# Paged attention on one Trainium2 core: opening with register-addressed copies of the conditions' weights, mixed input transposed by VectorE, last projection in two halves

## The chip, the cores and the metric

The kernel runs on one core of one Trainium2 chip. The metric is the device time of an execution in microseconds (us), lower is better. A core has five engines that run side by side and wait for each other through semaphores: TensorE (PE, with its weight loads PEld), VectorE (DVE), ScalarE (ACT), GpSimd (POOL) and SyncE (SP). SP, ACT and POOL also issue DMA copies, each in its own queue.

## What is computed

Two layers with residuals, on 64 sequences of 32 tokens and 512 channels, all in 32-bit floats. The first mixes the 32 tokens of a sequence with one of 16 weight tables of 32x32, chosen by the sequence's condition. The second is attention with 32 query heads and 8 key/value heads of 128 over a paged cache of 512 keys, of which the first `cache_seqlens` are valid, plus the 32 new tokens.

```python
x = x + einsum('bct,bcd->bdt', x, weights[condition])
q, k, v = x @ Wq.T, x @ Wk.T, x @ Wv.T          # q: 32 heads, k and v: 8
q, k = rope(rmsnorm(q)), rope(rmsnorm(k))
k_all = concat(k_cache[block_table], k); v_all = concat(v_cache[block_table], v)
probs = softmax(where(valid, q @ k_all * scale, -1e30))
x = x + (probs @ v_all) @ Wo.T
```

## The kernel before

The work is cut into 32 steps. A step is four sequences (128 token rows, BT = 4) with one half of the heads: steps 0 to 15 are all rows with heads 0 to 15 (`st.hh` = 0), steps 16 to 31 the same rows with the other heads. A step has four batches (its sequences), a batch four slots (its key/value heads), so a step has slots 0 to 15. In each slot PE makes the scores of one head group (`scores`, L570), ACT their exponential, and PE the product with the values of the slot before (`values`, L626). Between these lie, slot by slot, pieces of the next step: its key projection in slot 3 and query projections in 4 to 7, its v projection in 13 (`pieces`, L866), and the output projection of the step before in 8 and 9 (`out_proj`, L513). Two steps ahead, in slots 14 and 15, the rows are mixed and turned:

- `x1_c` (L359): PE multiplies the rows with `bd`, which holds the four sequences' weight tables on its diagonal (`pmix`), and DVE adds the product to the rows (`acc`).
- `x1_b` (L366): PE transposes the mixed rows in four blocks of 128x128 into PSUM (`px1t`), ACT copies them to `x1t`, the operand of the projections, and stores `x1t` in DRAM (`x1t_d`), from where the second half of the steps loads it (`x1_t`, L353).

The order of SP's queue and of PE's work is written by hand: they take what they have to do in the order of the program, over the whole kernel. In the opening (L766 to L864) that holds for all engines. SP issues the cached keys page by page (64 KB each, 16 a batch, two batches ahead, L294), the spreading of the turned queries (`spread`, L466), the loads and stores of the rows, and the weights; each batch's page numbers are first loaded into registers (L286). POOL gathers the cached values (`fetch`, L314, 256 KB each), which ACT masks (L334). The rotation of queries and keys (`norm_rope`, L412) runs on ACT, DVE and POOL; its products use the work buffer with tag `w1`, of which there is one.

The opening loads the condition of each row, from which DVE computes a row index, and POOL gathers the first step's weight tables with it (`w_sel`, L772). The index rows of the value gathers (`cached_rows`, L160) need `pages_at` and `lens_at`, which POOL loads after three weight loads. The first angles (`angles`, L133) are computed before the first mix, the second ones after `cached_rows`. `keep_warm` (L788) keeps PE busy with products of an identity. At the end, `in_range` (L1013) counts the usable denominators within the last output projection, and a branch runs an exact version if any is out of range.

## Time and profile before

| what | us |
|---|---|
| median of 3 runs | 2170.74 (2169.95 to 2174.28) |
| the profiled execution | 2166.54 |
| its span, first to last instruction | 2164.8 |
| PE busy | 2145.4 (99% of the span) |
| DVE / ACT / POOL busy | 1196.6 / 863.0 / 805.5 |

The profile is of one execution. Times in its views are counted from the first instruction. L12 is line 12 of the kernel. The chain of waits follows the work that ended last back to what released it. A matmul of 128x512 in 32-bit floats stands in it as two records of 0.43 us; a transpose of 128x128 as one of 0.11.

### The profile page before, as it was taken

To read this page: it belongs to the slowest core of one execution; us is meant where nothing else is said; L and a number is where in the kernel's file an instruction comes from. 1 tells how busy PE (TensorE), PEld (TensorE's weight loads), DVE (VectorE), ACT (ScalarE), POOL (GpSimd) and SP (SyncE) were. 2 spreads that over 40 slices of the span, in tenths; PEclk is the share of its full clock that TensorE was granted. 3 is DMA by queue.
4 is the path that set the end of the run, shared out by engine and by line. 5 is a ranking of instruction groups with operands and counts; after the bars stand their busy time and mean duration, and the time that the engine had idled before them with its cause. 6 is when DMAs were issued, how large, how long until landed. Compare 5 with 4: busy or idle time off the path is not lost.

```text
span 2164.8 us, 41582 instructions
## 1 busy us (share of the span) xinstructions
PE 2145.4 (99%) x12990; PEld 1497.4 (69%) x12990; DVE 1196.6 (55%) x2884; ACT 863.0 (40%) x1576; POOL 805.5 (37%) x1009
## 2 busy tenths in 40 slices
PE   8999999999999999999999999999999999999998
PEld 5766777667776677766777766777667777667775
DVE  5666555665455564555654565644655545556442
ACT  3444444444433343333443333433334433334441
POOL 4433333433333343333433334333334333334330
PEclk9999999999999999999999999999999999999999
DMA  8665565555655556556766855565555555555651
GB/s 250 188 165 160 157 169 160 143 159 158 173 153 153 154 156 173 156 151 190 229 181 178 207 161 162 164 177 156 155 144 168 165 167 165 147 159 162 172 158 59
DMA packets 386839, 357.47 MB, mean 165 GB/s; under 512 B 54480, under 2 KB 316640, under 8 KB 386608
## 3 DMA queue, kind: packets, MB, share of 16 engines
q1 hardware_dynamic: 341616, 212.74, 35.1%
q0 software_dynamic: 41984, 137.71, 22.3%
q10 hardware_dynamic: 3008, 4.25, 0.5%
q8 instruction: 106, 1.74, 0.3%
q14 instruction: 125, 1.02, 0.2%
HBM read 302.59 MB, written 12.58 MB: 146 GB/s over the span
## 4 chain that ended last, share of the span: by engine, by line
PE 97%; DVE 1%; DMA 1%; ACT 0%; issue 0%; POOL 0%; DVEq 0%; ACTq 0%
PE po_x L632 22%; PE ps_x L574 21%; PE pout_x L520 20%; PE pp_q_x L407 20%; PE pp_v_x L407 5%; PE pp_k_x L407 5%; PE pnv_x L616 2%; PE psn_x L592 1%; PE pmix_x L363 1%; DMA pages_at<-in_pages_v_dram 1%; PE px1t_x L371 0%; DMA cond<-in_cond_dram 0%; PE pt_x L451 0%; ACT sq_q_x L417 0%; ACT q_cols_x L491 0%
## 5 line engine op out<-in xcount | busy, mean ns | idle before, releaser
L321 POOL DMA_INDIRECT raw_x<-in_vc_dram,v_row x512 | 539.6, 1054 | 821.5 <-ACT v_x L334 757.0
L582 ACT ACTIVATE pr_x<-ps_x 128x512 f32<-128x512 f32 x512 | 305.7, 597 | 822.7 <-PE ps_x L574 819.3
L632 PEld LDWEIGHTS po_x<-v_x,pr_x 128*128 128x128 f32 x4096 | 515.7, 192 | 123.9 <-issue 112.5
L632 PE MATMUL po_x<-v_x,pr_x 128*128 128x129 f32 x4096 | 550.6, 278 | 0.0
L407 PE MATMUL pp_q_x<-wq_x,x1t_x 128*128 128x512 f32 x1024 | 462.2, 594 | 0.0
L520 PE MATMUL pout_x<-wo_x,ot_x 128*128 128x512 f32 x1024 | 450.2, 593 | 0.0
L574 PE MATMUL ps_x<-q_cols_x,kh_x 128*128 128x128 f32 x3072 | 406.0, 275 | 1.6 <-ACT q_cols_x L491 1.6
L574 PEld LDWEIGHTS ps_x<-q_cols_x,kh_x 128*128 128x128 f32 x3072 | 376.3, 192 | 18.0 <-issue 14.5
L334 ACT ACTIVATE v_x<-raw_x,valid 128x512 f32<-128x512 f32 x512 | 363.2, 716 | 13.4 <-DMA raw_x<-in_vc_dram,v_row 13.2
L520 PEld LDWEIGHTS pout_x<-wo_x,ot_x 128*128 128x128 f32 x1024 | 190.0, 191 | 214.0 <-issue 213.8
L567 DVE COPY kh_x<-k_t_x 128x512 f32<-128x512 f32 x506 | 206.8, 418 | 194.6 <-PE ps_x L574 153.5
L407 PEld LDWEIGHTS pp_q_x<-wq_x,x1t_x 128*128 128x128 f32 x1024 | 185.8, 191 | 184.8 <-issue 184.8
L650 DVE TENSOR_TENSOR nv_x<-po_x,nv_x 128x258 f32<-128x258 f32 x256 | 108.6, 424 | 309.4 <-PE po_x L632 294.0
L424 POOL TENSOR_TENSOR rs_q_x<-ms_q_x,minus_half 128x4 f32<-128x4 f32 x128 | 140.0, 1094 | 168.9 <-DVE ms_q_x L422 168.9
L417 ACT ACTIVATE sq_q_x<-pp_q_x 128x512 f32<-128x512 f32 x128 | 76.4, 597 | 266.2 <-PE pp_q_x L407 179.3
L574 PE MATMUL ps_x<-q_last_x,kh_x 128*128 128x128 f32 x1024 | 135.3, 275 | 0.0
L528 DVE TENSOR_TENSOR acc_x<-pout_x,acc_x 128x512 f32<-128x512 f32 x32 | 22.2, 692 | 199.3 <-PE pout_x L520 199.3
L574 PEld LDWEIGHTS ps_x<-q_last_x,kh_x 128*128 128x128 f32 x1024 | 124.6, 192 | 0.0
L407 PE MATMUL pp_v_x<-wv_x,x1t_x 128*128 128x512 f32 x256 | 115.2, 593 | 0.0
L407 PE MATMUL pp_k_x<-wk_x,x1t_x 128*128 128x512 f32 x256 | 115.1, 593 | 0.0
L653 DVE TENSOR_TENSOR o_x<-nv_x,rden 128x256 f32<-128x256 f32 x256 | 108.8, 425 | 6.2
L421 DVE TENSOR_REDUCE ms_q_x<-sq_q_x 128x4 f32<-128x512 f32 x128 | 86.3, 674 | 45.4 <-ACT sq_q_x L417 44.8
(107 smaller groups left out, 1464.8 us busy)
## 6 DMA issues: line engine op xcount, KB each, us to landing
k_t_x<-in_kt_dram SPq DMA_DIRECT2D x2048, 64.0 KB
q_cols_x<-rows_x SPq DMA_DIRECT2D x360, 80.0 KB
q_last_x<-rows_x SPq DMA_DIRECT2D x120, 80.0 KB
raw_x<-in_vc_dram,v_row POOLq DMA_INDIRECT x512, 4.2
wo_x<-in_wo_dram SPq DMA_DIRECT2D x32, 256.0 KB
acc_x<-in_x_dram SPq DMA_DIRECT2D x16, 256.0 KB
x1t_d<-x1t_x ACTq DMA_DIRECT2D x16, 256.0 KB
acc_d<-acc_x SPq DMA_DIRECT2D x16, 256.0 KB
```

What stands on the lines that cost most here:

```text
L321: nc.gpsimd.indirect_dma_start(out=raw.rearrange("p g d -> p (g d)"), out_offset=None, in_=vc, in_offset=bass.IndirectOffsetOnAxis(ap=v_ro ...
L334: nc.scalar.activation(v_bufs[b % 2][:, c, :, 0:D], raw, AF.Copy, scale=ok)
L407: nc.tensor.matmul(pp, st.x1t[:, c, :], w[:, c, :], start=(c == 0), stop=(c == KC - 1))
L421: nc.vector.tensor_reduce(ms, sq, AX.X, ALU.add)
L424: nc.gpsimd.tensor_tensor(rs, ms, minus_half, ALU.pow)
L520: nc.tensor.matmul(st.po, st.ot[:, i, :], wt["o", st.hh, i // 4][:, i % 4, :], start=(i == 0), stop=(i == QH - 1),)
L567: last["dve"] = nc.vector.tensor_copy(k, ba.k_raw[:, :, g, :]).ins
L574: nc.tensor.matmul(ps[:, c, :], ba.k[g][:, c * P : (c + 1) * P], queries(ba, g), start=True, stop=True,)
L582: last["act"] = nc.scalar.activation(pr, ps, AF.Exp, scale=SCALE).ins
L632: nc.tensor.matmul(ba.po[:, g % 2, :], ba.pr[g][:, c, :], ba.v_t[:, c, g, :], start=(c == 0), stop=(c == VC - 1),)
L650: nc.vector.tensor_tensor(t, ba.po, t, ALU.add)
L653: nc.vector.tensor_tensor(ba.o[:, both, :], t[:, :, 0:D], rd.unsqueeze(2).to_broadcast([P, 2, D]), ALU.mult,)
```

## The change

- **Opening, conditions.** `cond_0`, its index and the gather of `w_sel` go. ACT's first copy is now the condition row, its second the page numbers. SP loads all 16 weight tables (`w_all`, 64 KB) after the first rows. DVE loads the first step's four conditions into registers and copies four 32x32 blocks addressed by them. The tables of step 1 are loaded by SP instead of ACT.
- **Opening, order of loads.** The second quarter of wq goes from POOL to SP. `pages_at` and `lens_at` go from POOL to ACT. The fourth quarter of wq and the second batch of keys come after step 1's tables.
- **Opening, order of work.** The first mix comes before the angles. The second angles are split: DVE's part (`reduced`) before the first query projection, ACT's part (`sines`) after it, followed by an exponential of one column. Some projections, gathers, copies, scores and values change places. The first `x1t` is stored by POOL, later. There are fewer warming products (10, 4 and 3 instead of 16, 6 and 4).
- **Steps 2 to 15.** The mixed rows are no longer transposed by PE. DVE turns their 32x32 blocks (`x1_turn`), SP writes them to `x1t_d` with four DMAs, which put the blocks in place in pieces of 32 floats, and at the start of the next step SP loads `x1t` back, after the first four key pages of a batch and before the other twelve.
- **End.** The last output projection is made in two halves of 256 columns, each with its own addition and store; `in_range` is called within the first.

```diff
@@ steps_of: x1 @@
         def x1_b(st):
             if st.hh:
                 return
+            if not by_tensor(st):
+                return x1_turn(st)
...
             nc.scalar.copy(st.x1t, pm)
-            nc.scalar.dma_start(x1t_d[st.t], st.x1t.rearrange("p c q -> p (c q)"))
+            if st.n or exact:
+                keep_x1t(st, nc.scalar)
...
+        def x1_turn(st):
+            turned = work.tile([P, KC * BT, S], F32, tag="w1", name=f"x1w_{st.name}", bufs=1)
+            nc.vector.transpose(turned, st.acc.rearrange("p (j d) -> p j d", d=S))
+            kept = x1t_d[st.t].rearrange("(j d) (c b x) -> b d c j x", d=S, b=BT, x=S)
+            for b in range(BT):
+                nc.sync.dma_start(
+                    kept[b],
+                    turned[b * S : (b + 1) * S, :, :].rearrange("p (c j) x -> p c j x", c=KC),
+                )
@@ out_proj @@
-                nc.vector.tensor_tensor(st.acc, st.po, st.acc, ALU.add)
+                nc.vector.tensor_tensor(st.acc[:, cols], st.po[:, cols], st.acc[:, cols], ALU.add)
                 if exact or st is steps[-1]:
-                    store(st)
+                    store(st, cols)
@@ opening: loads @@
-            nc.scalar.dma_start(cond_0, cond[:, 0:1])
-            nc.vector.tensor_scalar(cond_0, cond_0, float(S), row, ALU.mult, ALU.add)
-            nc.gpsimd.dma_start(pages_sb, pages)
+            nc.scalar.dma_start(cond_row, cond.rearrange("(i s) t -> s t i", s=S)[0:1])
+            nc.scalar.dma_start(pages_sb, pages)
...
         x1_a(first)
+        w_all = work.tile([S, NCOND, S], F32, tag="pr", name="w_all", bufs=3)
+        nc.sync.dma_start(w_all, w_cond.rearrange("(n s) e -> s n e", s=S))
         load_w("q", 0, 0)
+        load_w("q", 0, 1)
         nc.scalar.dma_start(lens_sb, lens)
         nc.scalar.dma_start(freq, inv_freq.partition_broadcast(P))
...
         load_w("k", 0, eng=nc.gpsimd)
-        load_w("q", 0, 1, eng=nc.gpsimd)
+        nc.scalar.dma_start(pages_at, pages_v)
+        nc.scalar.dma_start(lens_at, lens_row.partition_broadcast(P))
         load_w("q", 0, 2, eng=nc.gpsimd)
         batch = Batch(first, 0)
         load_w("v", 0)
         x1_a(second)
-        load_w("q", 0, 3)
-        later = Batch(first, 1)
...
         keep_warm(WARM)
+        number = conditions(0, mybir.EngineType.DVE)
+        for i in range(BT):
+            blk = slice(i * S, (i + 1) * S)
+            nc.vector.tensor_copy(
+                bd[blk, blk], w_all[:, bass.ds(number[i], 1), :].rearrange("p o e -> p (o e)")
+            )
+        x1_c(first)
+        load_cond_weights(1)
+        load_w("q", 0, 3)
+        later = Batch(first, 1)
         positions()
         angles(0, trig)
-        for i in range(BT):
-            nc.vector.tensor_copy(bd[blk, blk], w_sel[blk, :])
-        x1_c(first)
-        keep_warm(6)
+        keep_warm(4)
         x1_b(first)
-        load_cond_weights(1, nc.scalar, mybir.EngineType.Activation)
-        keep_warm(4)
+        keep_warm(3)
         rot_tables(first)
...
         cached_rows(pages_at, lens_at)
-        angles(TRIG, trig)
-        for c in range(RAW):
-            fetch(0, c)
-        fetch(0, RAW, tag="pn", bufs=1)
+        reduced(TRIG, trig)
         q_a(first, 0)
+        sines(TRIG, trig)
+        nc.scalar.activation(early, half_pi, AF.Exp)
+        fetch(0, 0)
+        fetch(0, 1)
         k_a(first)
+        fetch(0, 2)
+        keep_x1t(first, nc.gpsimd)
         q_a(first, 1)
+        fetch(0, RAW, tag="pn", bufs=1)
@@ opening: further on @@
-        k_b(first)
+        new = v_product(first)
+        q_b(first, 1)
         for c in (0, 1):
             batch.fill(c)
             fetch(1, c)
-        v_a(first)
-        q_b(first, 1)
+        v_copy(first, new)
...
         x1_b(second)
-        scores(batch, 2)
...
         q_b(first, 3)
+        scores(batch, 2)
         scores(batch, 3)
...
         values(batch, 1)
+        values(batch, 2)
         new_values(first, 2)
@@ loop over the steps @@
+                back = bt == 0 and ahead and not ahead.hh
...
+                        NPP // 4 if back else NPP // 2 if bt == BT - 1 else NPP,
+                    if back:
+                        x1_t(ahead)
+                        for load in after.pages_left:
+                            load()
...
-                        if beyond:
+                        if beyond and beyond.hh:
                             x1_t(beyond)
@@ end @@
-        out_proj(steps[-1], slice(0, QH), in_range)
+        out_proj(steps[-1], slice(0, QH), slice(0, HID // 2), in_range)
+        out_proj(steps[-1], slice(0, QH), slice(HID // 2, HID))
```

## The prediction

> **What bounds the kernel now.** I read the page's busy shares first (PE 99%), then the windows by stage, since an average over the run hides the two ends.

> ```profile
> 0.00:62.00 62.00, 52.14 (x269) 34.34 (x270) 32.87 (x94) 23.71 (x52) 26.11 (x46) 0.94 0.80 232
> 62.00:2100.00 2038.00, 2038.00 (x12406) 1424.07 (x12405) 1146.19 (x2742) 821.73 (x1494) 770.03 (x952) 1.00 0.59 166
> ```

> The columns are the stretch in us, its length, busy time of PE, weight loads, DVE, ACT and POOL, the granted clock, the DMA engines' share and GB/s. From 62 us on TensorE has no idle time at all and full clock; DVE is at 56%, ACT 40%. So in that stretch only PE work that goes away, or a new PE stall, changes the time. What is idle on PE lies in the first 62 us, where the DMA engines are at 0.80, and in the last 10. The chain of waits tells why the opening idles:

> ```profile
> 7.71 11.25 DMA pages_at<-in_pages_v_dram
> ...
> 19.06 0.35 DVE v_row L164
> ...
> 23.06 0.31 ACT sin L150
> ...
> 24.00 0.49 ACT sq_q_x L417
> ...
> 42.77 3.73 issue
> ...
> 59.13 1.54 PE pnv_x L616 x16
> ```

> The copy of pages_at stands behind 3 MB of weights in POOL's queue, lands at 18.96, and holds DVE (index rows, then the second pair of angles), which holds the sines on ACT, which hold the first square, although its projection was over at 18.9. From there DVE's norm-and-rotate chain (3.65 us for each of q0, k, q1, q2) and ACT set the pace. The step's own part, in the same view around a step boundary, and the SP queue beside it in the timeline:

> ```profile
> 233.33 0.86 PE pmix_x L363 x2
> ...
> 235.97 0.44 PE px1t_x L371 x4
> ...
> 247.37 3.44 PE pp_k_x L407 x8
> ```
> ```profile
> 227.09 0.53 SPq L351 DMA_DIRECT2D acc_x<-in_x_dram  x1
> 229.05 8.44 SPq L294 DMA_DIRECT2D k_t_x<-in_kt_dram  x16
> ```
> ```profile
> 241.77 5.93 SPq L294 DMA_DIRECT2D k_t_x<-in_kt_dram  x11
> ```

> The four transposes of the mixed input cost PE 0.44 us a step, and 11.4 us later the key projection needs the result. SP is late at this point: it issues the 16 key pages of slots 12 and 13 one every 0.54 us until 237.5, past the end of slot 15. The end:

> ```profile
> 2151.61 3.65 PE pout_x L520 x8
> ...
> 2155.27 0.69 DVE acc_x L528
> ```

> [...] The new stores write 128 B pieces. The trace before has no such write; its 128 B reads (bd) took 12 ns a packet in the trace's packet records, the 512 B key pages 27, the 2 KB stores of x1t_d 87. [...] beside the 1 MB of wq, three small copies issued by ACT within 0.9 us landed at 3.82 (cond), 5.27 (lens) and 7.02 (freq)[...]. [...] STREAM_TRANSPOSE of 128x512 takes 0.70 us here. [...] 0.66 in the window 10 to 15 us, after PE's 3.2 us of idling before pmix.

> **Steps 2 to 15: the transposes.** 14 steps lose four PE transposes: 14 x 0.44 = **-6.2 us**, all on the path, since PE is never idle there. A cross-check: a first-half step takes 67.13 us (projection of the output at 205.44, next at 272.57), a second-half step 65.83 (1405.96 to 1471.79); the difference of 1.30 is pmix 0.86 plus 0.44. ACT loses its copy (0.58) and one store. DVE gains 0.70 us a step; it was idle from 236.5 to 240.3, which hides it. The tile shares tag w1 with the rotation's; the next user is the key's rotation at 252, long after the stores have read it. The x1t buffer that the load fills was last read by v's projection, over by 231.6.

> What is added on SP: four stores (64 KB in 512 pieces each), and in the next step the load, which waits for all four; behind it on SP wait 12 key pages. Those have room: SP's queue sat idle on its buffers from 262.5 to 269.7 in this step, and the keys are needed a batch later. The load itself has not. From 237.5: stores at 0.6 each (the spread copies of L471, 80 KB each, come every 0.62; bounds 0.35, as the old store, and 0.9) 2.4; the page-number load 1.1; four pages 2.1, which makes 243.1. The stores have landed by then if they take under 3.8 us after the last issue at 239.3 (the old store was issued at 237.18 and SP, which waited for it, went on at 241.77: at most 4.6). The load of 256 KB: a gather of the same size lands in a median 4.1 us in this stretch, of which 1.0 is its own issue; 3.1, bounds 2.4 and 4.1. So x1t is there at 246.2, and k's projection wants it at 247.37 - 0.44 = 246.9. Bounds: 2.4 us early (0.35, 2.4), 2.0 late (0.9, so a last issue at 240.2, a store of 4.6, 4.1). I take it as in time in most steps and late in some, 0.3 us on the mean: 14 x 0.3 = **+4.2 us**.

> **The opening.** The condition row is now ACT's first copy, so it lands like cond did, at 3.9. DVE's register load isn't in the trace: SP's of the same row takes 0.30, ACT's 0.51; I take 0.5, with all of DVE queued behind it and pmix waiting. Four 32x32 copies of 0.17 with their register moves, 1.0. The weight table itself (64 KB, second on SP) should land with the condition row. So pmix starts at 5.9 instead of 10.07. Then freq binds: fourth on ACT's queue, beside SP's two 1 MB loads and POOL's, at 9.5 (bounds 7.0, as now, and 11). Angles 2.3 on DVE, sines 0.9 and the x1t copy 0.6 on ACT: first projection at 13.5 instead of 15.34. It may run at half clock for a time, +1. pages_at and lens_at leave POOL's queue for the fifth and sixth place on ACT's, 16 (12 to 17) instead of 18.96 and 19.2; index rows 2.0 and reduction 2.0 follow. The first square no longer waits for sines, so the q0 chain on DVE starts at 19.5 instead of 24.52. The exp table (1.28 us, in the chain at 36.37) is loaded early, under q0's chain. From there PE's written order at 3.44 per projection, ACT's four value fills and v's copy (3.4 us behind q1's columns) give: q3's projection at 39 (42.82), the second step's k at 44.5 (48.52; the scores that stood before it are moved behind), and with values of head 2 put under the copies that PE waited for at 58.1, the second step's q0 at 55.6 instead of 61.60: **-6.0 us**, bounds -9 (freq at 7, full clock) and -2. SP gains wq1 and bd's four copies and loses nothing, so it runs about 2 us earlier, not 6; the last page of its third batch of keys was issued 14 us before use (60.3, 74.3), which covers that. Storing the first x1t on POOL (one issue of 0.8) lies before gathers that have slack. Fewer warming matmuls cost nothing by themselves; their loss is the half clock above.

> **The tail.** Two halves of 32 records of 0.215 make the same 13.7. The last add covers 256 columns, 0.42 instead of 0.69 (nv_x 128x258 takes 0.42), and the last store half the bytes: **-0.5 us** (0 to -1). The count of denominators moves earlier; DVE was done with it at 2143.9, before PE gets there at about 2146.

> **Sum.** -6.2 + 4.2 - 6.0 - 0.5 = -8.5. The profiled execution took 2166.54 around its span of 2164.8, so 2158.0 there; the median shown is 2170.74, so **2162.2**. A measurement of this kernel can tell about 0.2% (4.3 us) from no change.

> **Rivals.** *The load of x1t comes late, and the kernel is slower.* Place: SP's queue between slot 15 and slot 3 of the next step; PE takes its work in order, so each us late is a us of stall, 14 times. It ends even at (6.2 + 6.0 + 0.5) / 14 = 0.9 us per step and is slower by over 0.2% from 1.2. At 1.5 us (stores 0.9 apart that land as slowly as the old one, load 3.6): 2170.7 - 12.7 + 21 = 2179. For it: the margin of 0.7 us rests on two latencies that this trace doesn't show. Against: the DMA share there is 0.52 (240 to 247), and 128 B packets are cheap. *The opening's gain is lost to the DMA engines.* They are saturated (about 345 GB/s) from 10 to 20 and 25 to 35 us; if ACT's small copies get their turn only at the end of the weights, the chain starts 2 us earlier, not 5: 2170.7 - 6.2 + 4.2 - 2 - 0.5 = 2166.2. *The transposes don't go to the path* can be excluded: PE has no idle time.

> **How the numbers follow.** Forecast (2157 to 2166) 0.60, of it 0.56 faster. Opening hidden (2164 to 2169) 0.22, of it 0.09 faster, 0.13 same. Load late (2168 to 2190) 0.18: 0.04 same, 0.14 slower. With 0.04 same from the first: faster 0.65, same 0.21, slower 0.14. The range reaches from all bounds good short of the extremes, 2157, into the late case, 2174.

> **What would show it.** Right: PE's wait list still empty after 60 us, first-half steps of 66.7 us, second step's q0 near 55.6, freq landing under 10. Wrong: PE waiting for x1t_x from x1t_d at L407 in first-half steps (late load), or the first pmix, the first square or q0's rows not earlier (opening). A DVE transpose scheduled late, or pages_at landing after 18, would break the sums above.

## The result, and the profile after

The changed kernel takes **2186.26 us** (median of 6 runs, 2180.74 to 2190.92), the kernel before 2171.56 beside it: ratio 1.0072, 95% interval 1.0061 to 1.0082. That is slower by 0.7%, some 15.6 us, where 8.5 us less were forecast. Its profiled execution took 2185.52 us, with a span of 2183.7 against 2164.8.

The windows of the kernel after, with the same columns as the first fence of the prediction: stretch, length, busy time of PE, weight loads, DVE, ACT and POOL, granted clock, DMA share, GB/s.

```profile
0.00:62.00 62.00, 52.06 (x256) 32.63 (x257) 32.60 (x93) 25.28 (x55) 24.78 (x43) 0.94 0.78 232
62.00:2100.00 2038.00, 2020.22 (x12180) 1404.26 (x12180) 1147.60 (x2737) 808.37 (x1460) 760.02 (x943) 1.00 0.59 166
```

Where PE had no idle time from 62 us on, it now idles for 17.8 us. What it waits for is in its list of waits from 62 to 2160 us (us in total, times, longest), which was empty before:

```profile
PE pp_k_x L436 <- DMA x1t_x<-x1t_d: 14.3, 8, 2.9
PE pp_k_x L436 <- ACT v_x L346: 1.9, 2, 1.0
PE pp_k_x L436 <- ACT nv_x L657: 1.5, 3, 0.7
```

All three are the same place, the key projection of steps 2 to 15; in the last two the view names another engine that ended shortly before, but the matmul records show the same gap ahead of the same projection, 14 times in 14 steps. Counted from the first matmul of the mixing, the projection starts 0.3 to 3.1 us later than before, 20.0 us in all; the idle time of the windows is 2.2 us less, because the records of two matmuls in a row overlap by 0.16 us where nothing waits. The SP queue at the boundary whose lines the prediction shows, in the timeline of the kernel after (start, length from the first issue to the last, line, copy, how many):

```profile
232.20 0.53 SPq L363 DMA_DIRECT2D acc_x<-in_x_dram  x1
234.05 9.04 SPq L306 DMA_DIRECT2D k_t_x<-in_kt_dram  x16
243.19 3.08 SPq L400 DMA_DIRECT2D x1t_d<-x1w_x  x4
248.01 1.91 SPq L306 DMA_DIRECT2D k_t_x<-in_kt_dram  x4
250.11 0.33 SPq L368 DMA_DIRECT2D x1t_x<-x1t_d  x1
```

And PE at the end of it, where the bracket gives its idle time and the releaser:

```profile
252.87 3.67 PE L436 MATMUL pp_k_x<-wk_x,x1t_x 128*128 128x512 f32 x8 [0.84 <-DMA x1t_x<-x1t_d]
```

VectorE's transpose was done at 240.84. The stores stand behind 16 pages until 243.2; between 246.3 and 248.0 SP reads the next page numbers; then come four pages, and the load leaves at 250.1, 9.3 us after its data were ready. One step earlier the chain of waits has the same course, with a longer wait:

```profile
172.40 0.57 SPq L400
173.02 0.88 SPq L400
173.95 2.88 DMA x1t_d<-x1w_x
...
179.51 3.76 DMA x1t_x<-x1t_d
183.40 5.37 PE pp_k_x L436 x8
```

The chain puts 2.88 us to the landing of a store, but by SP's records these us are the fourth store's issue (174.62, 1.50 us) and the load of the page numbers (176.16, 0.99 us). In the whole first half SP's list of waits has 1.5 us for the landing of the stores ahead of the load: the queue sets the time, not the landing. The key projection takes 5.37 us here, not 3.67. Windows around it show why; the column after POOL's is the granted clock:

```profile
180.00:183.40 3.40, 0.50 (x5) 0.33 (x4) 0.00 (x0) 1.47 (x4) 0.95 (x1) 1.00 0.84 254
183.40:188.60 5.20, 5.20 (x8) 2.19 (x9) 0.00 (x0) 0.00 (x0) 0.00 (x0) 0.67 0.54 158
```

After 2.9 us without work the granted clock is 0.50 from 184.1 to 187.5 us (single matmuls go from 0.59 to 1.06 us), so the wait costs a second time. The opening, in the timeline of the kernel after:

```profile
12.34 0.29 DVE L142 TENSOR_TENSOR trig<-freq,pos 128x128 f32<-128x128 f32 x1 [1.74 <-DMA freq<-in_inv_freq_dram]
...
14.43 0.31 ACT L158 ACTIVATE sin<-trig 128x128 f32<-128x128 f32 x1 [7.50 <-DVE trig L153]
...
15.28 0.56 ACT L386 COPY x1t_x<-px1t_x 128x512 f32<-128x512 f32 x1
...
15.90 5.86 PE L436 MATMUL pp_q_x<-wq_x,x1t_x 128*128 128x512 f32 x8 [6.46 <-ACT x1t_x L386]
```

The mixed rows were turned by 8.8, but ACT's copy of them stands behind the sines, these behind freq. PE idles for 6.5 us, then starts the first projection half a microsecond later than before, at half clock (0.50 from 13.5 to 20.3 us). The second step's q0 starts at 59.59 (61.60 before).

The table splits the span's 18.9 us, by matmul starts in both traces. The wait's part comes from the output projection that starts at 1027.26 after and 1010.80 before: 16.5 later, 2.0 of opening and 6.2 of transposes gained, so 24.6 lost.

| part | forecast | trace |
|---|---|---|
| opening, to the second step's q0 | -6.0 | -2.0 |
| 14 x four transposes | -6.2 | -6.2 |
| late x1t: 20.0 until the key projections start, the rest slow key projections | +4.2 | +24.6 |
| second half, 65.9 us a step instead of 65.83 | 0 | +1.2 |
| last step, up to its last output projection | 0 | +1.9 |
| tail, from there to the end | -0.5 | -0.6 |
| sum | -8.5 | +18.9 |

### The profile page after: what moved, and what is told of

It reads as the page before. It is cut to its first block, busy times and chain, and to the rows that moved or that the text cites. A ratio compares the mean times of both kernels' runs of the same rounds, so it can differ in the third digit from the quotient of the medians.

```text
span 2183.7 us, 41707 instructions
## 1 busy us (share of the span) xinstructions
PE 2145.9 (98%) x12948; PEld 1497.1 (69%) x12948; DVE 1205.3 (55%) x2898; ACT 861.6 (39%) x1563; POOL 801.3 (37%) x1005
## 4 chain that ended last, share of the span: by engine, by line
PE 91%; SPq 3%; DMA 2%; issue 1%; ACT 1%; DVE 0%; DVEq 0%; ACTq 0%
PE pout_x L554 20%; PE pp_q_x L436 20%; PE ps_x L607 19%; PE po_x L665 19%; PE pp_k_x L436 5%; PE pp_v_x L436 4%; PE pnv_x L649 2%; SPq L306 2%; PE psn_x L625 1%; DMA x1t_x<-x1t_d 1%; DMA x1t_d<-x1w_x 1%; SPq L500 0%; SPq L400 0%; DMA k_t_x<-in_kt_dram 0%; PE pmix_x L374 0%
## 5 line engine op out<-in xcount | busy, mean ns | idle before, releaser
L554 PE MATMUL pout_x<-wo_x,ot_x 128*128 128x512 f32 (+1 forms) x1056 | 450.5, 580 | 0.5 <-DVE acc_x L562 0.5
L607 PEld LDWEIGHTS ps_x<-q_cols_x,kh_x 128*128 128x128 f32 x3072 | 376.1, 192 | 16.5 <-issue 16.0
L554 PEld LDWEIGHTS pout_x<-wo_x,ot_x 128*128 128x128 f32 x1056 | 195.7, 190 | 210.0 <-issue 207.6
L436 PE MATMUL pp_k_x<-wk_x,x1t_x 128*128 128x512 f32 x256 | 120.8, 616 | 18.7 <-DMA x1t_x<-x1t_d 14.3
L562 DVE TENSOR_TENSOR acc_x<-pout_x,acc_x 128x512 f32<-128x512 f32 (+1 forms) x33 | 22.3, 676 | 204.8 <-PE pout_x L554 204.8
L450 DVE TENSOR_REDUCE ms_k_x<-sq_k_x 128x4 f32<-128x512 f32 x32 | 22.0, 686 | 171.5 <-ACT sq_k_x L446 171.5
```

The lines of the kernel that those rows point to most:

```text
L436: nc.tensor.matmul(pp, st.x1t[:, c, :], w[:, c, :], start=(c == 0), stop=(c == KC - 1))
L554: nc.tensor.matmul(st.po[:, cols], st.ot[:, i, :], wt["o", st.hh, i // 4][:, i % 4, cols], start=(i == 0), stop=(i == QH - 1),)
L607: nc.tensor.matmul(ps[:, c, :], ba.k[g][:, c * P : (c + 1) * P], queries(ba, g), start=True, stop=True,)
```

## The experiments

The theory (A): the loss is the wait for x1t, and that comes from its place in SP's queue. Rivals: the way through DRAM is slow wherever it is issued, or the new work disturbs others. The medians of the kernel before that stood beside the runs differ (2166.8 to 2171.6), so ratios to it are compared; 0.1% is 2.2 us.

**e1, the opening and tail alone.** TensorE transposes again, and nothing is loaded back in the first half.

```diff
-            if not by_tensor(st):
-                return x1_turn(st)
...
-                back = bt == 0 and ahead and not ahead.hh
+                back = False
```

> The changed kernel with TensorE's transposes put back in steps 2 to 15 (and ScalarE's copy and store), so that no load of x1t stands ahead of the first half's key projections: the new opening and the halved last projection alone. Theory A (the whole loss is the late x1t): in the changed kernel's trace the steps 2 to 15 lost 24.7 us to the wait and to what follows it and saved 6.2, so this kernel takes 2186.3 - 18.5 = 2168, within 2165 to 2171, with no wait of PE ahead of the key projection and first-half steps of 67.13 us. Rival B (the rearranged opening or the tail, or a different schedule of ScalarE and VectorE in the long middle, costs too): over 2174.

2164.92 us, ratio 0.9979 (0.9972 to 0.9986): 0.92% under the changed kernel, 20 us, and just below the range of theory A. No wait ahead of a key projection; first-half steps of 67.13 us but for two of 67.15 and 67.29. So the loss sits in the middle part, and opening and tail alone are a small gain over the kernel before, 4.6 us.

**e13, the middle part alone,** on the kernel before: `x1_turn`, its stores and the load behind four pages, as the change has them.

> The kernel before with the middle part of the change alone: VectorE's transpose, four stores by SP behind slot 15's queue and the load behind four key pages, in steps 2 to 15; the old opening and the old tail. Theory A (the middle part alone makes the loss; opening and tail are a small gain beside it): 24.7 us of lateness less 6.2 of transposes over the kernel before, ratio 1.0085, so about 2188 where before takes 2169.5; within 1.006 to 1.011. Rival F (the lateness comes from the new opening, which puts PE ahead of SP's queue): a ratio under 1.004, with gaps ahead of the key projection only in some steps.

2183.39 us, ratio 1.0077 (1.0063 to 1.0091). PE's waits from 62 us on:

```profile
PE pp_k_x L421 <- DMA x1t_x<-x1t_d: 16.3, 12, 3.4
```

The same loss without the new opening: rival F is out. With e1's, the two parts make +12.1 us against +15.6 for both, within the intervals. The second half of this kernel runs at 65.83 a step.

**e3, the new work without the load and its wait.** Both ways run side by side: TensorE's result is used, VectorE's is stored. (The expectation counts the writes double: 14 x 4 stores in 512 pieces are 28672 pieces, 3584 KB.)

```diff
             if not by_tensor(st):
-                return x1_turn(st)
+                x1_turn(st)
...
-            if st.n or exact:
+            if st.n == 1 or exact:
                 keep_x1t(st, nc.scalar)
...
-                back = bt == 0 and ahead and not ahead.hh
+                back = False
```

> TensorE's transposes make the first half's x1t as in the kernel before, but VectorE's transpose and its four stores by SP are kept as well and make the copy in DRAM that the second half reads; no load in the first half. So all work of the new way is there, and its wait isn't. Theory A (the wait alone costs): the same time as e1, about 2168, within 2 us of it. Rival B2 (the 128 B writes, 7168 KB in 57344 pieces... or SP's 2.5 us of issues per step delay gathers, keys or exponentials that PE then waits for): 3 us or more above e1, with PE waiting on something else than x1t.

2165.46 us, ratio 0.9985 (0.9978 to 0.9992), 1.3 us over e1 with overlapping intervals. The 128 B writes, SP's four issues and VectorE's transpose displace nothing that shows in the time. The load itself stays untested here; in e11 and e12 it is there without a wait.

**e8, the load ahead of the pages.** The smallest edit to the place in the queue.

```diff
-                            NPP // 4 if back else NPP // 2 if bt == BT - 1 else NPP,
+                            0 if back else NPP // 2 if bt == BT - 1 else NPP,
```

> The changed kernel with x1t's load issued ahead of all key pages of the batch instead of behind the first four; nothing else. Theory A1 (each us that SP comes to the load sooner is a us less of waiting, until the stores' landing binds, some 3 us after the last one is issued): the load goes out 1.2 us sooner where the stores have landed, the gaps shrink by about 1 us each, 14 us in all: about 2172, within 2168 to 2178. Rival A2 (the stores' landing already binds): within 3 us of 2186.

2165.45 us, ratio 0.9993 (0.9985 to 1.0002): 17 us less than the changed kernel's 1.0072, no different from the kernel before, and better than the 2168 to 2178 that A1 expected. At the boundary shown above the load is now issued at 246.86, and PE starts the key projection at 249.69 without a gap. What is left of the waits:

```profile
PE pp_k_x L436 <- DMA x1t_x<-x1t_d: 4.0, 2, 2.5
```

These are steps 2 and 3, where SP is latest. So four pages were most of the loss. Counted from the mixing, the load leaves 0.9 us sooner on the mean (11.0 instead of 12.0 us), not the 1.2 that was expected, because it now waits for the stores to land: SP's list has 26.9 us of that in the first half, where the change has 1.5. The way through DRAM is thus the next bound behind the queue, and an earlier load alone can't gain more.

**e2, the stores on ScalarE's queue.**

```diff
-                nc.sync.dma_start(
+                nc.scalar.dma_start(
                     kept[b],
```

> The changed kernel with the four stores of the transposed input issued by ScalarE instead of by SP. Theory A1 (what makes x1t late is its place in SP's queue: behind 16 key pages that SP issues late, then four store issues, a page-number load and four pages ahead of the load): the stores leave right after VectorE's transpose, the load is issued some 3 us earlier, the gaps of 0.3 to 3 us ahead of the key projection go, and the time is about 2186.3 - 24 = 2162, within 2158 to 2167. Rival A2 (the way through DRAM takes the time itself: writes of 128 B pieces land so late that the load waits for them wherever they are issued): gaps stay above half their size and the time above 2174. Rival C: ScalarE pays 4 issues of 0.6 us in front of its exponentials, and PE waits for those instead: 2166 to 2176 with PE waiting on ScalarE's pr or v.

2206.46 us, ratio 1.017 (1.0156 to 1.0184), 21 us worse than the change. A1 as I put it failed here. The signs of A2 are there (over 2174, gaps above half), but they don't speak for it, since the load wasn't issued earlier at all: 12.0 us after the mixing on the mean, as in the change. PE's two longest entries:

```profile
PE pnv_x L649 <- ACT pn_x L633: 24.6, 21, 3.2
PE pp_k_x L436 <- DMA x1t_x<-x1t_d: 7.6, 7, 2.7
```

That is rival C's place, but not by the issue time alone. SP's own list of waits in the first half:

```profile
SPq L306 <- DMA x1t_d<-x1w_x: 45.4, 14, 3.9
```

In the traces before and after, SP's and ACT's copies take their completion semaphores from one set of eight, in turn: a key page whose turn falls on the semaphore of one of ACT's stores waits until that has landed, 3.2 us a step. ACT's fourth store waited in the same way for its second (issued at 247.61, the second landed at 247.59), with exponentials behind it. In the kernel before, the old store on ACT's queue held SP for 26.7 us in 14 steps by this; in the change that entry is gone.

**e6, the mixing four slots earlier.** The input is loaded at slot 5, mixed and turned at 10 and 11, x1t loaded at 13.

```diff
-            st.acc = work.tile([P, HID], F32, tag="acc", name=f"acc_{st.name}", bufs=3)
+            if st.n % 4 == 3 and not exact:
+                st.acc = rows[:, 0, 0:4, :].rearrange("p g d -> p (g d)")
+            else:
+                st.acc = work.tile([P, HID], F32, tag="acc", name=f"acc_{st.name}", bufs=3)
...
-                        if slot == 11:
+                        if slot == 5:
                             x1_a(beyond)
...
-                    if slot == 14 and beyond:
+                    if slot == 10 and beyond:
                         x1_c(beyond)
-                    if slot == 15 and beyond:
+                    if slot == 11 and beyond:
                         x1_b(beyond)
```

> The changed kernel with the input for the step after next loaded at slot 5 (11 before), mixed at slot 10 (14), transposed by VectorE and stored by SP at slot 11 (15), and x1t loaded at slot 13, ahead of that slot's key pages, as in the second half; so that a fourth input fits, each fourth one lies in the tile of rows, unused by then. The way through DRAM stays the same, only its place in SP's queue is earlier. Theory A1 (the loss is the place in SP's queue): no wait for x1t, first-half steps of 66.7 us, e1's 2164.9 less 14 x 0.44 = 2158.7, within 2156 to 2162. Rival A2 (the way through DRAM is slow in itself, some 10 us from VectorE's transpose to PE, or SP's 2.5 us of store issues displace keys wherever they stand): waits remain, for x1t or keys, and the time is over 2165.

2169.19 us, ratio 1.0012 (1.0006 to 1.0019), not the 2158.7 expected. The borrowed tile was not unused: the spreading of the queries reads it in every step, so every fourth step computes with overwritten rows and the early steps wait for it; the step after the first takes 74.98 us. The other first-half steps take 66.69 to 67.3 us with no gap over 0.15 us ahead of a key projection, as A1 says, but as a total this run tells nothing.

**e11, the same work in another order,** with no buffer added.

```diff
-                back = bt == 0 and ahead and not ahead.hh
+                back = False
...
                     if slot == 10 and st.n:
                         store(steps[st.n - 1])
+                        if beyond:
+                            x1_a(beyond)
...
                     if slot == 13:
-                        if beyond and beyond.hh:
-                            x1_t(beyond)
-                        for load in after.pages_left if after else ():
-                            load()
-                    if slot == 14 and beyond:
-                        x1_c(beyond)
-                    if slot == 15 and beyond:
-                        x1_b(beyond)
+                        if beyond:
+                            x1_c(beyond)
+                            x1_b(beyond)
+                        left = after.pages_left if after else []
+                        if beyond and not beyond.hh:
+                            for load in left[:4]:
+                                load()
+                            left = left[4:]
+                        if beyond:
+                            x1_t(beyond)
+                        for load in left:
+                            load()
```

> The changed kernel with the same work in another order on SP: the next input is loaded at slot 10, right behind the store; mixed, transposed and stored at slot 13, ahead of that slot's 8 key pages instead of behind them; x1t is loaded after the first 4 of these pages. Theory A1 (the place in SP's queue is the loss): no wait for x1t but perhaps in the first two steps, first-half steps of 66.69 us; e1's 2164.9 less 14 x 0.44 = 2158.7, within 2156 to 2163. Rival A3 (SP has no room: the keys that now come 3 us later are waited for, by VectorE's copies and then PE): a gap of the same size moves to the scores, and the time stays over 2165.

2162.80 us, ratio 0.9970 (0.9959 to 0.9981). SP at the same boundary, to be read beside the change's:

```profile
226.38 3.97 SPq L306 DMA_DIRECT2D k_t_x<-in_kt_dram  x8
232.06 2.65 SPq L400 DMA_DIRECT2D x1t_d<-x1w_x  x4
234.90 2.02 SPq L306 DMA_DIRECT2D k_t_x<-in_kt_dram  x4
237.76 0.33 SPq L368 DMA_DIRECT2D x1t_x<-x1t_d  x1
```

The load leaves 7.1 us ahead of its key projection (244.85); no wait for x1t anywhere; first-half steps of 66.69 to 66.80 us. A1 holds, and A3 doesn't: the later keys aren't waited for. The total is 2.1 us under e1's, where 6.2 were expected. Part of that is in the trace, whose execution was the slowest of the seven (2167.45): in step 17 the store of the rows took SP 2.1 us to issue, the new load of the rows behind it waited until 1230.7 for that store to land, the spreading behind them came late, and that step took 72.14 us. In e12's trace, with the same order, the step took 65.99 us. How often this happens in the other executions no run shows.

**e4, the first x1t copied ahead of the sines.**

```diff
-        angles(0, trig)
         keep_warm(4)
         x1_b(first)
         keep_warm(3)
+        angles(0, trig)
```

> The changed kernel with the first x1t copied out of PSUM ahead of the sines on ScalarE (and written ahead of the angles), so that the first projection needs no freq. Theory D (the opening gained 2 us, not 6, because the copy stood behind the sines at 15.3 us and wq0 had landed at 13.4): the first projection starts at 13.4 to 13.6 instead of 15.9, the first square and q0's chain 2.3 us earlier, the second step's q0 at 57.3 instead of 59.6, total 2.3 us less than the changed kernel less the noise of the x1t waits. Rival E (the sines or later weights, wk at 16.9 and wq1 at 21.1, set the pace): first projection earlier, but the second step's q0 within 0.5 us of 59.6.

```profile
11.92 3.67 PE L436 MATMUL pp_q_x<-wq_x,x1t_x 128*128 128x512 f32 x8 [2.44 <-DMA wq_x<-in_wq_dram]
```

2186.60 us, ratio 1.0082 (1.0068 to 1.0095). The first projection starts 4.0 us earlier, now at full clock and bound by its weights (here 11.9; in the trace of after the last of them landed at 13.4), and the second step's q0 2.5 us earlier, at 57.12; the total doesn't move. The first wait for x1t grew instead, from 2.8 to 4.0 us, and the key projection behind it now ran at half clock, 1.7 us longer; the first output projection starts at 139.29 (138.85 in the change). What PE gains, SP's late load takes.

**e9, e1 with the same edit.**

> e1 (TensorE's transposes in all first-half steps) with the first x1t copied ahead of the sines, as in e4. No late x1t can eat what the opening gains. Theory D2 (in e4 the 2.5 us gained in the opening were lost to SP's late load, not to the opening itself): 2164.9 - 2.5 = 2162.4, within 2161 to 2164. Rival E2 (something else behind the opening takes them back, such as SP's keys or ScalarE's fills): within 0.7 us of e1.

2163.28 us, ratio 0.9975 (0.9965 to 0.9986). The second step's q0 at 57.12 against e1's 60.98, and the fourteenth output projection at 1007.57 against 1010.51, so 2.9 of 3.9 us arrive in the traces, where e4's gained nothing. The medians differ by 1.6 us, by the ratios 0.9, which is too little to tell D2 from E2 by time.

**e12, e11 with the same edit.**

> e11 with the first x1t copied ahead of the sines. If both theories hold (A1 and D2), the gains add: 2158.7 - 2.5 = 2156, within 2154 to 2160, 0.6% under the kernel before. If SP is what stands behind an earlier opening (E2), it stays within 1 us of e11, with the wait for x1t or keys in the first steps growing by what the opening gains.

2161.22 us, ratio **0.9960** (0.9947 to 0.9974): 0.4% faster than the kernel before, 1.1% faster than the change. That is above the 2154 to 2160 expected, and 1.6 us under e11, between D2 and E2. In the traces the opening's gain stays: the first output projection starts 3.1 us earlier than e11's, the fourteenth 3.2. From 62 us on PE is without idle time again:

```profile
62.00:2100.00 2038.00, 2038.00 (x12415) 1424.59 (x12415) 1166.42 (x2766) 824.46 (x1489) 769.16 (x954) 1.00 0.60 168
```

**e10, e6 with the same edit,** has e6's fault, and like it tells nothing as a total: 2169.59 us, ratio 1.0010 (1.0003 to 1.0016).

> e6 with the first x1t copied ahead of the sines, as in e4. In e4 the second step's q0 came 2.5 us earlier (57.1 against 59.6) and the total didn't move; theory D2 says that SP's late load ate that, since SP's queue is no earlier in e4. Without that wait the gain must arrive: e6 less 2.5 us, about 2156. Rival E2 (SP's keys or ScalarE's fills behind the opening set the time, so an earlier q0 is lost anyway): within 0.7 us of e6.

**e5, the kernel before once more.**

> The kernel before, unchanged, with a new profile: its first profiled execution (2166.5 us) lies below all of its 37 timed runs in the last comparison (2167.7 to 2171.6), so a comparison of traces with it may be some 3 us too hard on the changed kernel. If the difference is spread over the run, it shows in the periods of the steps; if it comes from the opening, the second step's q0 starts 2 to 4 us later than 61.6.

2168.33 us, ratio 1.0001 (0.9992 to 1.0010). Its profiled execution took 2168.46: the second step's q0 at 62.30 instead of 61.60, the first output projection 1.6 us later, all steps after it equal within 0.01 us. So the first profile had a quick opening, and against this one the change's opening gained 2.7 us, not 2.0.

## Why the prediction was wrong

**Which way it went.** The first rival happened, at its place and by its mechanism: the load of x1t comes late, and PE, which works in order, stalls for it 14 times. It was priced at 1.5 us a step and 2179 us; it cost 24.6 / 14 = 1.76. Of the two latencies that it named, the landing of the stores cost next to nothing (1.5 us in all) and the load took 3.0 us, not 3.6; what made it late is the queue. The chance of 0.18 was too small, and the range's end of 2174 fell short of a case that the text itself had priced.

**The transposes (-6.2)** were right: in e8, whose steps 4 to 15 hardly wait, the output projections of some steps are 67.13 - 0.44 = 66.69 us apart.

**The step that failed** is "I take it as in time in most steps and late in some, 0.3 us on the mean". Term by term, from the first matmul of the mixing (233.17 in the trace before) to x1t's landing, as means of the 14 steps:

| term | put at | measured |
|---|---|---|
| to the first store | 4.3 | 4.9 |
| four stores | 2.4 | 3.1 |
| page numbers and four pages | 3.2 | 4.0 |
| load, issue to landing | 3.1 | 3.0 |
| sum | 13.0 | 15.0 |
| wanted by PE | 13.6 | 13.6 |

So it was late by 1.4 on the mean, in every step by 0.3 or more, and 14 x 1.43 = 20.0. No term is far off: a store's issue took 0.77 us instead of 0.6 and was inside its bounds; 16 pages took 9.04 us instead of 8.44; the page-number load up to 1.4 instead of 1.1. But three terms of one serial queue erred in the same direction, against a margin of 0.7 us. The 0.3 took the bounds, 2.4 early to 2.0 late, as scatter between steps. They were mostly doubt about values that come again in all steps: a store that takes 0.77 us to issue on the mean takes it 14 times. So the chances should have been shared between a cost of next to nothing and one of over 1 us a step rather than put on the mean. The load's own latency, one of the two that the trace before didn't show, was right.

**A cost left out.** The prediction counts a slower clock in the opening, not after the wait. Its 0.66 for 10 to 15 us is the granted clock of the trace before, which was 0.50 from 11.5 to 14.9, behind PE's 3.2 us of idle time. In the change two of the 14 key projections ran for 3.4 us at 0.50, and 1.7 us longer than the others, after 2.6 and 2.9 us of idle time. With 0.07 us in each of the 14 (3.51 instead of 3.44 from their start to the next work) that makes 4.4 of the 4.6 us beyond the late starts.

**The opening (-6.0)** gained 2.0 to 2.7. pmix at 5.9 was right (5.98). Then freq was put at 9.5 and landed at 12.3, past its bound of 11: ACT's six copies landed at 3.9, 9.4, 10.1, 12.3, 14.9 and 17.2, where the trace before had four at 3.8, 5.3, 6.9 and 8.7. By the packet records SP's queue moved 1272 KB and POOL's 228 KB from 2.0 to 8.5 us in the trace before, 1436 and 588 KB from 2.0 to 12.0 in the change. The first projection came at 15.9 instead of 13.5, and at half clock (0.50), 2.3 us longer; the text had 1 for that. The q0 chain on DVE began at 22.4 instead of 19.5, the second step's k at 47.1 instead of 44.5, its q0 at 59.6 instead of 55.6. That wq0 landed only at 13.4 the prediction left out; with freq in time, it would have been the bound. The second rival (2 us from the opening) had the size right. e4 shows that 2.5 us of what was missing lay in the order on ACT.

**The tail (-0.5)** was -0.6 in the trace, although PE waits 0.52 us between the halves for the first half's add. No run measured it by itself.

**The places that were to show it:** PE's wait list isn't empty, the first-half steps aren't 66.7 us, q0 isn't near 55.6 and freq isn't under 10; what was named as the sign of the rival, PE waiting for x1t_x from x1t_d in first-half steps, is what the trace shows.

**Left open:** the 1.2 us of the second half (65.9 in the change, e1, e9, e11 and e12, 65.83 in e8 and e13, whose second halves do the same work) and up to 1.9 us in the last step (1.9 again in e1, 0.1 in e8, 0.5 in e12). In the last step PE has 1.4 us of idle time ahead of scores and values in the change, and 1.7 ahead of values in e1. What shifts either wasn't found.

## What to carry to other kernels

Replacing work on the bounding engine by a way through DRAM means buying a deadline: add up the whole serial queue that the copies pass, every store, register load and page ahead of the load, and price the sum's upper half, because early counts nothing and late counts each time, with the clock on top (here 1.7 us in two of 14 steps). If the margin is smaller than the spread of the sum, move the copies first: four pages moved behind the load gave back 17 us here, and e11's order brought first-half steps of 66.7 us, the transposes' gain. An opening's gain that runs ahead of another queue is not yet a gain; look at which queue PE meets next.
